# Another order of the Mamba state, its replicated loads, and VectorE's token operations interleaved

## The chip, the cores and the metric

The kernel runs on one core of one Trainium2 chip. A core has TensorE (PE) for matmuls, VectorE (DVE), ScalarE (ACT) and GpSimd (POOL) for work on elements, and SyncE (SP), which here issues nearly all DMA transfers. Each engine works through its own queue in order; semaphores join the queues. The metric is the device time of one execution in microseconds. Times of single instructions come from one profiled execution.

## The reference, cut to what matters

Four layers follow one another on x of shape (2, 128, 128, 128) in float32. Layers 0 and 2 are the same: a 3x3 convolution, then a Mamba scan in which the 128 channels of a pixel are a sequence of 8 tokens of 16 features, then a group norm, SiLU and a residual. Layer 1 gates x by a density of windows, and layer 3 is a residual block of two 3x3 convolutions with batch norm. The change lies in the scan:

```python
y = conv3x3(x, conv_w) + conv_b
seq = y.reshape(B * H * W, 8, 16)                    # 8 tokens of 16
xi, z = split(seq @ in_proj_w.T)                     # 32 channels each
xc = silu(causal_conv1d(xi))                         # over the tokens
dt, Bm, Cm = split(xc @ x_proj_w.T, [1, 17])         # Bm, Cm: 16 states
dt = softplus(dt @ dt_proj_w.T + dt_proj_b)
dA = exp(dt[..., None] * A)                          # 32 channels x 16 states
dBx = dt[..., None] * Bm[:, :, None, :] * xc[..., None]
h = a * h + b                                        # token by token
ys = sum(h * c[:, None, :], axis=-1)                 # over the 16 states
out = ((ys + D * xc) * silu(z)) @ out_proj_w.T
```

For each pixel and token there are thus 32 x 16 = 512 numbers of state.

## The kernel before, in words

The Mamba layers go through the image in tiles of four rows, 512 pixels (NS), 64 tiles a layer and 128 in all. The pixels lie along the free dimension. The 512 state numbers of a pixel are 128 partitions times 4 free groups (NJ = 4): the 32 channels are split in four groups of eight (DJ = 8, index e), and the 8 channels x 16 states of a group fill the partitions. Which partition holds channel e and state n is told by `_state(e)` (line 72). In the kernel before, states 0 to 15 of channels 0 to 6 lie at n * 7 + e, and channel 7 fills the last 16 partitions. The constants `neg` and `red` and the weights `alog` are built from the same function on the host.

Per tile k and token t the work of the scan is:

- `load` (429, SP): u = dt * xc and the pair (B, C) of the token lie in DRAM scratch (`su`, `sb`) and are read back replicated over the partitions, into `ur` (4 x 512 elements a partition, three buffers) and `bcr` (2 x 512, five buffers). Lines 435 and 439 read for the first 112 partitions, lines 436 and 440 for the last 16.
- `inject` (442, GpSimd): h(t) = ur * B, line 445, into one of four buffers.
- `decay` (447, TensorE and ScalarE): four small matmuls (line 454) spread dt * A over the partitions into two PSUM tiles named `set`, one for each half of the free groups; line 463 takes the exponential in place. There are three `set` buffers for two tiles a token, so the tiles take turns, and one that is needed again must have been read for the last time.
- `token` (465, VectorE), for each half: line 472 multiplies `set` by h(t-1) in place, line 473 multiplies the product by C into `r`, and line 477 adds the product to h(t). Below these three are called d, w and u, with the half behind: d0, w0, u0, d1, w1, u1. Token 7 has no u, and token 0 is handled apart.
- `gather` (485, TensorE): line 492 sums `r` over the states into the PSUM tile `ys`, one for four tokens; `through` (479, line 483) begins each `ys`, and `gate` (501, line 505, VectorE) takes it, twice a tile. `out` (507, line 512, TensorE) then projects, and `spread` (522) gathers statistics.

The work on the other tiles that fills the gaps is the convolution (line 323), the projections (350), dt (364, 365), softplus (368), B and C (400, 407), their product (412, GpSimd), `own` (420, 421), u (374, GpSimd), `own_u` (425 to 427) and the stores (382, 389).

The order is written by hand. Each piece of work has a place on a line of tokens: tile k's token t stands at 7k + t - 1 and so on; `put` (line 554) notes it, and everything is sorted by place and issued in that order on every engine. The places that matter here: the token operations at t - 1 for half 0 and t - 0.5 for half 1, `decay` of token t at t - 1.2, `gather` at t + 0.35, the gates at 3.79 and 7.39, `through` at 1.25 and 4.2, `out` at 7.9. In a steady tile TensorE's queue therefore has, between the matmuls of one token's `decay` and the next: for tokens 2 to 3 `out` and the second `own` of neighbouring tiles, `through`, two taps of a convolution and a `gather`; for tokens 5 to 6 two and a half projections, a `through` and a `gather`; the others have less or have waits on ScalarE in them.

Of the kernel before, what the change touches and what calls it, by code (L numbers as in the profile page):

```python
# [27 lines left out]
ALU = mybir.AluOpType  # L28
# [3 lines left out]
P = 128  # L32
NT, FT = 8, 16
DI, DS, DC = 32, 16, 4
NQ = 4
NJ = DI * DS // P
DJ = DI // NJ
NG = 4
CG = P // NG
WIN = 8  # L40
ROWS = 4
NS = ROWS * P
# [7 lines left out]
def _constants(H):  # L50

    parts = {}

    neg = np.zeros((NJ, NQ, DJ, NQ, P), np.float32)
    red = np.zeros((P, NQ, NQ, DJ), np.float32)
    gsum = np.zeros((2, NQ, DS, 2, NJ, NQ, DJ), np.float32)
    for q in range(NQ):
        for e in range(DJ):
            neg[:, q, e, q, _state(e)] = -1.0
            red[_state(e), q, q, e] = 1.0  # L60
        for g in range(2):
            gsum[g, q, :, g, :, q, :] = 1.0
    parts["neg"] = neg.reshape(P, -1)
    parts["red"] = red.reshape(P, -1)
    parts["gsum"] = gsum.reshape(P, -1)
    parts["group"] = np.kron(np.eye(NG), np.full((CG, CG), 1.0 / CG)).astype(np.float32)
    parts["ident"] = np.eye(P, dtype=np.float32)
    parts["neghalf"] = np.full((P, CG), -0.5, np.float32)
    return _packed(parts)


def _state(e):


    return np.arange(DS) + P - DS if e == DJ - 1 else np.arange(DS) * (DJ - 1) + e


def _bilinear(n):
# [38 lines left out]
def _mamba_layout(w):  # L117
# [5 lines left out]
    def half(a):  # L123

        a = a.reshape(*a.shape[:-2], 2, NQ, NJ, DJ)
        return np.ascontiguousarray(np.swapaxes(a, -3, -2)).reshape(*a.shape[:-4], 2 * P)
# [18 lines left out]
    for q in range(NQ):  # L145
        pdt1[:, q, :, :, q, :] = by_d[0][:, :, None, None]
        pdt2[:, q, :, :, q, :] = w["dt_proj_w"][:, 0].reshape(NJ, DJ)[None, None, :, :]
        pb[:, q, :, q, :] = by_d[1 : 1 + DS].transpose(1, 2, 0)
        pc[:, q, :, q, :] = by_d[1 + DS :].transpose(1, 2, 0)
        for e in range(DJ):  # L150
            alog[:, q, e, q, _state(e)] = w["A_log"].reshape(NJ, DJ, DS)[:, e, :]
# [128 lines left out]
STORE_AT = -4.15  # L280
LOAD_AT, INJECT_AT = -3.7, -1.8
REP_AT = -1.2
SUM_AT = 0.35
D_AT = (1.25, 4.2)
V_AT = (3.79, 7.39)
# [3 lines left out]
def _mamba(tc, src, w, con, dst, scratch, stats, H):  # L289


    nc = tc.nc
# [11 lines left out]
    live = {}  # L304
# [124 lines left out]
    def load(k, t):  # L429

        s = live[k]
        n = P - DS
        ur = s["ur", t] = st.tile([P, NJ, NS], F32, tag="ur", name="ur", bufs=3)
        u = s["su"][t]
        nc.sync.dma_start(out=ur[:n], in_=u[: DJ - 1].unsqueeze(0).to_broadcast([DS, DJ - 1, NJ, NS]))
        nc.sync.dma_start(out=ur[n:], in_=u[DJ - 1].unsqueeze(0).to_broadcast([DS, NJ, NS]))
        m = s["bc", t] = st.tile([P, 2, NS], F32, tag="bcr", name="bcr", bufs=5)
        b = s["sb"][t]
        nc.sync.dma_start(out=m[:n], in_=b.unsqueeze(1).to_broadcast([DS, DJ - 1, 2, NS]))
        nc.sync.dma_start(out=m[n:], in_=b)  # L440

    def inject(k, t):
        s = live[k]
# [18 lines left out]
        for x in a:  # L462
            nc.scalar.activation(x, x, AF.Exp)  # L463

    def token(k, t, jp):

        s = live[k]
        if jp == 0:
            s["r", t] = st.tile([P, NJ, NS], F32, tag="r", name="r", bufs=2)
        pt = s["a", t][jp]  # L470
        js = slice(2 * jp, 2 * jp + 2)
        nc.vector.tensor_tensor(pt, pt, s["h", t - 1][:, js, :], ALU.mult)  # L472
        nc.vector.tensor_tensor(  # L473
            s["r", t][:, js, :], pt, s["bc", t - 1][:, 1].unsqueeze(1).to_broadcast([P, 2, NS]), ALU.mult
        )
        if t < NT - 1:
            nc.vector.tensor_tensor(s["h", t][:, js, :], pt, s["h", t][:, js, :], ALU.add)  # L477

    def through(k, g):

# [66 lines left out]
    x1, z1 = ahead(1)[0], behind(1)[0]  # L547
    order = [(0, band)] + taps(0, 0, 9) + [(0, turn)] + x0 + taps(1, 0, 3) + dt0 + taps(1, 3, 5) + bc0
    order += [(0, load, 0), (0, load, 1), (0, load, 2)]
    order += z0 + taps(1, 5, 9) + [(1, turn), (0, decay, 1), (0, inject, 0), (0, inject, 1)] + own0  # L550
    order += x1[:2] + z1[:2]
    early = {x: n - 100.0 for n, x in enumerate(order)}

    def put(k, at, f, *args):
        at = early.get((k, f, *args), k * SPAN + at)
        todo.append((at, len(todo), f, (k, *args)))


    for k in range(len(src) * ntile):
        if k * ROWS % BAND == 0:  # L560
            put(k, BAND_AT, band)
        for tap in range(9):
            put(k, CONV_AT[tap], conv, tap)
        put(k, TURN_AT, turn)
        for n in range(4):
            put(k, IN_AT[n], project, *divmod(n, 2))
        for name in ("xc", "zs"):
            put(k, SILU_AT, silu, name)
        for i in range(2):
            put(k, BC_AT[i], inout, i)  # L570
        for g in range(2):
            put(k, DT_AT[g], step, g)
        put(k, SOFTPLUS_AT, softplus)
        put(k, PROD_AT, product)
        put(k, U_AT, scaled)
        for g in range(2):
            put(k, OWN_AT[g], own, g)
        put(k, OWN_U_AT, own_u)
        put(k, STORE_AT, store)
        for t in range(NT - 1):  # L580
            put(k, LOAD_AT + t, load, t)
            put(k, INJECT_AT + t, inject, t)
        for t in range(1, NT):
            put(k, REP_AT + t, decay, t)
            for jp in range(2):
                put(k, t - 1 + jp / 2, token, t, jp)
            put(k, SUM_AT + t, gather, t)
        for g in range(2):
            put(k, D_AT[g], through, g)
            put(k, V_AT[g], gate, g)  # L590
        put(k, OUT_AT, out)
        put(k, STATS_AT, spread)
        put(k, KEEP_AT, keep)
# [26 lines left out]
def _gates(tc, src, w, con, y, stats, wm, b1, up, dst, H):  # L620
# [6 lines left out]
    with tc.tile_pool(name="dg", bufs=2) as dp, tc.tile_pool(name="dg1", bufs=1) as sp, tc.tile_pool(  # L627
# [58 lines left out]
        def gram(b, y0):  # L686
# [3 lines left out]
            pg = s["pg"] = psg.tile([P, 2, 512], F32, tag="pg", name="pg")  # L690
            tiles = [(a, a * P // 2, g * CG) for g in range(NG) for a in range(2)]
            for a, pa, c0 in tiles:
# [335 lines left out]
def _program(ctx, tc, d, cols, out):  # L1028
# [7 lines left out]
    with tc.tile_pool(name="const", bufs=1) as cp, tc.tile_pool(name="wts", bufs=1) as wp:  # L1036
        cc = cols["const"]
        ct = cp.tile([P, cc["neghalf"][1]], F32, tag="ct", name="ct")
        nc.sync.dma_start(out=ct, in_=d["const"])
        con = {k: ct[:, a:b] for k, (a, b) in cc.items()}  # L1040
        w1 = cp.tile([P, CG], F32, tag="w1", name="w1")
        nc.sync.dma_start(out=w1, in_=d["w1t"])
        w2 = cp.tile([CG, 2 * P + P // 2], F32, tag="w2", name="w2")
        nc.sync.dma_start(out=w2, in_=d["w2b"])
        b1 = cp.tile([CG, 1], F32, tag="b1", name="b1")
        nc.sync.dma_start(out=b1, in_=d["b1"])
        wm = {"w1": w1, "w2": w2[:, :P], "b2": w2[:, P : 2 * P], "one": w2[:, 2 * P :]}

        y = [dram.tile([P, H, P], F32, tag=f"y_{b}", name=f"y_{b}") for b in range(B)]

        def layer(src, n):
            w = _layer_weights(nc, wp, {k: d[f"L{n}_{k}"] for k in ("conv", "fold", "alog", "keep")}, cols[n], con)
            stats = wp.tile([P, B, H // ROWS, 6], F32, tag="stats", name="stats")
            _mamba(tc, src, w, con, y, scratch, stats, H)
            return w, stats

        x = [d["x"][b] for b in range(B)]
        w, stats = layer(x, 0)
        _gates(tc, x, w, con, y, stats, wm, b1, d["up"], x2, H)
        w, stats = layer(x2, 2)  # L1060
        with tc.tile_pool(name="ps_n", bufs=1, space=PSUM) as pp:
            norm = [_norm(nc, npool, pp, w, con, stats, b) for b in range(B)]
# [44 lines left out]
```

## Time and profile before

| | |
|---|---|
| median of 3 runs | 7580.34 us (7578.54 to 7589.2) |
| span of the profiled execution | 7571.5 us |
| difference of the two | 8.8 us |
| first Mamba layer, first d to last | about 57 to 3310 us |
| second Mamba layer, first d to last | about 3655 to 6900 us |
| DMA busy share, 1000 to 3000 us | 0.97, at 250 GB/s |
| VectorE busy, 1000 to 3000 us | 1928.0 of 2000 us |
| mean granted TensorE clock | 0.929 |

The span runs from the first to the last instruction. The two Mamba layers are some 86% of it, and a tile takes about 50 us in them. Busy times count an engine's own work, not its waits; a matmul's end is modelled. A row such as "L472 DVE ... x1792 | 2193.5, 1224 | 267.6 <-ACT set L463 165.4" reads: line 472 on VectorE ran 1792 times, was busy for 2193.5 us, took 1224 ns on average, and VectorE stood idle for 267.6 us just before these instructions, 165.4 of it ended by ScalarE's line 463. In a row of order in time the first number is the start and the second the duration, both in us, and equal neighbours are merged.

### The profile page before, as it was taken

The page shows a single profiled execution, that of the slowest core. Times are in us where ns is not written, and L with a number is a line of the kernel's source. Part 1 is how long each engine was busy: PE and PEld are TensorE (multiplying, and loading weights), DVE is VectorE, ACT ScalarE, POOL GpSimd, SP SyncE. Part 2 cuts the span into 40 slices and gives each one's busy share as a digit, 9 for nine tenths or more (in the row PEclk, how much of TensorE's full clock was granted, in tenths as well). Part 3 has the DMA queues.
Part 4 walks back from the last instruction along what each step waited for, and adds up shares of the span by engine and source line. Part 5 has one row for each costly group of instructions (what it writes and reads, how often), then busy time and mean ns, then how long its engine had stood idle before and what let it go on. Part 6 is the DMA issues. An engine that isn't in the chain of part 4 may idle for free.

```text
span 7571.5 us, 89536 instructions
## 1 busy us (share of the span) xinstructions
PE 6319.0 (83%) x30416; PEld 2335.1 (31%) x30416; DVE 7011.8 (93%) x7114; ACT 4282.3 (57%) x4877; POOL 5499.8 (73%) x1783
## 2 busy tenths in 40 slices
PE   7888888888888888867788888888888888887994
PEld 2222222222222222224222222222222222223873
DVE  5999999999999999978699999999999999999986
ACT  5666666666656656545556666666656655662222
POOL 5878777877787778754578777877787778775541
PEclk8999999999999999978899999999999999997997
DMA  8999999999999999954799999999999999996604
GB/s 204 252 251 252 251 250 246 256 251 253 246 248 254 250 243 249 245 194 173 193 249 247 250 250 249 250 256 246 249 252 252 251 245 253 249 253 199 207 7 172
DMA packets 573738, 1769.80 MB, mean 234 GB/s; under 512 B 85568, under 2 KB 239712, under 8 KB 458208
## 3 DMA queue, kind: packets, MB, share of 16 engines
q1 hardware_dynamic: 568672, 1747.28, 88.1%
q10 hardware_dynamic: 4608, 16.78, 0.6%
q8 instruction: 242, 3.96, 0.2%
q14 instruction: 216, 1.77, 0.1%
HBM read 1552.83 MB, written 210.89 MB: 233 GB/s over the span
## 4 chain that ended last, share of the span: by engine, by line
DVE 41%; DMA 25%; PE 19%; issue 7%; ACT 5%; POOL 2%; SPq 1%; POOLq 0%; DVEq 0%; ACTq 0%
DMA bcr<-sb 19%; DVE set L472 14%; DVE h L477 12%; DVE r L473 12%; PE m L911 6%; DMA ur<-su 3%; PE one L350 2%; PE set L454 2%; ACT set L463 2%; PE ys L492 2%; PE one L400 2%; POOL h L445 2%; DVE v L505 1%; PE ys L483 1%; ACT xc L357 1%
## 5 line engine op out<-in xcount | busy, mean ns | idle before, releaser
L445 POOL TENSOR_TENSOR h<-ur,bcr 128x2048 f32<-128x2048 f32 x896 | 4060.7, 4539 | 1257.0 <-DMA bcr<-sb 1096.1
L472 DVE TENSOR_TENSOR set<-set,h 128x1024 f32<-128x1024 f32 x1792 | 2193.5, 1224 | 267.6 <-ACT set L463 165.4
L473 DVE TENSOR_TENSOR r<-set,bcr 128x1024 f32<-128x1024 f32 x1792 | 2194.5, 1225 | 61.5
L463 ACT ACTIVATE set<-set 128x1024 f32<-128x1024 f32 x1792 | 1745.9, 1006 | 870.0 <-PE set L454 856.6
L477 DVE TENSOR_TENSOR h<-set,h 128x1024 f32<-128x1024 f32 x1536 | 1866.0, 1215 | 28.1 <-POOL h L445 27.8
L454 PE MATMUL set<-dt,rep 32*128 32x512 f32 x7168 | 1402.9, 675 | 104.9 <-DVE h L477 98.1
L492 PE MATMUL ys<-r,ct 128*32 128x512 f32 x7168 | 1172.5, 635 | 36.4 <-DVE r L473 36.1
L323 PE MATMUL one<-band,conv 128*128 128x512 f32 x2304 | 1081.3, 605 | 21.9 <-DMA band<-in_x_dram 12.6
L454 PEld LDWEIGHTS set<-dt,rep 32*128 32x128 f32 x7168 | 405.1, 193 | 1002.3 <-issue 468.1
L400 PE MATMUL one<-xc,keep 128*64 128x512 f32 x1008 | 322.4, 723 | 462.1 <-ACT xc L357 355.5
L323 PEld LDWEIGHTS one<-band,conv 128*128 128x128 f32 x2304 | 406.6, 189 | 668.0 <-issue 596.8
L911 PE MATMUL m<-comb,u 128*128 128x256 f32 x2304 | 507.8, 381 | 46.0 <-DVE comb L904 44.8
L483 PE MATMUL ys<-t,ct 128*128 128x512 f32 x512 | 322.6, 716 | 252.3 <-DVE v L505 250.7
L911 PEld LDWEIGHTS m<-comb,u 128*128 128x128 f32 x2304 | 436.2, 190 | 117.3 <-issue 54.5
L492 PEld LDWEIGHTS ys<-r,ct 128*32 128x32 f32 x7168 | 181.2, 112 | 929.2 <-issue 759.6
L352 ACT ACTIVATE xc<-one,keep 128x512 f32<-128x512 f32 x252 | 173.4, 688 | 509.2 <-PE one L350 504.2
L374 POOL TENSOR_TENSOR u<-dt,xc 128x1024 f32<-128x1024 f32 x128 | 302.8, 2365 | 98.0 <-ACT dt L368 98.0
L420 PE MATMUL one<-prod,ct 128*128 128x512 f32 x504 | 280.8, 640 | 109.1 <-POOL prod L412 78.8
L350 PE MATMUL one<-y,w_in 128*128 128x512 f32 x504 | 341.1, 765 | 1.6 <-ACT xc L352 1.6
L463 ACT ACT_TABLE_LOAD x254 | 325.9, 1283 | 4.5
L427 POOL TENSOR_TENSOR t<-t,xc 128x1024 f32<-128x1024 f32 x128 | 302.4, 2363 | 10.0
L364 PE MATMUL one<-xc,w_dt 128*128 128x512 f32 x504 | 306.4, 692 | 2.7 <-ACT bc L407 2.7
(167 smaller groups left out, 5901.7 us busy)
## 6 DMA issues: line engine op xcount, KB each, us to landing
ur<-su SPq DMA_DIRECT2D x896, 896.0 KB, 11.5
bcr<-sb SPq DMA_DIRECT2D x896, 448.0 KB, 11.7
ur<-su SPq DMA_DIRECT2D x896, 128.0 KB, 11.1
su<-u SPq DMA_DIRECT2D x1024, 64.0 KB, 3.4
sb<-bc SPq DMA_DIRECT2D x256, 224.0 KB, 2.7
bcr<-sb SPq DMA_DIRECT2D x896, 64.0 KB, 11.0
y<-o SPq DMA_DIRECT2D x128, 256.0 KB, 9.3
band<-in_x_dram SPq DMA_DIRECT2D x28, 640.0 KB, 10.9
```

What stands on the lines that cost most here:

```text
L323: nc.tensor.matmul(py.rearrange("p (r w) -> p r w", r=ROWS), lhsT=w["conv"][:, tap, :], rhs=xb[:, r + kh : r + kh + ROWS, kw : kw + P], st ...
L350: nc.tensor.matmul(p, lhsT=w[("in", "z")[i]][:, g, :], rhs=s["y"], start=True, stop=True)
L400: nc.tensor.matmul(p[g * NQ * DS : (g + 1) * NQ * DS, :], lhsT=w[("xb", "xcm")[i]], rhs=s["xc"][:, g, :], start=True, stop=True,)
L445: nc.gpsimd.tensor_tensor(b, s["ur", t], s["bc", t][:, 0].unsqueeze(1).to_broadcast([P, NJ, NS]), ALU.mult)
L454: nc.tensor.matmul(a[j // 2][:, j % 2, :], lhsT=w["rep"][r, q, :], rhs=s["dt"][r, g, :], start=True, stop=True, tile_position=(r.start, 0),)
L463: nc.scalar.activation(x, x, AF.Exp)
L472: nc.vector.tensor_tensor(pt, pt, s["h", t - 1][:, js, :], ALU.mult)
L473: nc.vector.tensor_tensor(s["r", t][:, js, :], pt, s["bc", t - 1][:, 1].unsqueeze(1).to_broadcast([P, 2, NS]), ALU.mult)
L477: nc.vector.tensor_tensor(s["h", t][:, js, :], pt, s["h", t][:, js, :], ALU.add)
L483: nc.tensor.matmul(s["ys", g], lhsT=con["ident"], rhs=s["t1"][:, g, :], start=True, stop=False)
L492: nc.tensor.matmul(s["ys", g][a : a + NQ * DJ, :], lhsT=red[:, q, :], rhs=r[:, j, :], start=False, stop=(q == NQ - 1), tile_position=(0, a),)
L911: nc.tensor.matmul(m[:, n // 2, n % 2], lhsT=u[:, i, kw, :], rhs=v[:, i, :, kw : kw + P], start=(kw == 0), stop=(kw == 2),)
```

## The change

It has two parts. First, `_state` is another order: the 128 partitions are two halves of 64, one for channels 0 to 3 and one for channels 4 to 7; inside a half each state has four neighbouring partitions, one for each channel. `load` is rewritten to fit: bcr comes by two transfers of 32 partitions (eight states of the lower half each) and one of 64 (all 16 states of the upper half), ur by two of 64 partitions. They are issued in the order bcr 0 to 31, bcr 32 to 63, ur upper half, ur lower half, bcr upper half. That is five transfers a token where there were four, for the same bytes.

Second, `token` is cut in three functions with places of their own, so that VectorE's queue has d0, u1 of the token before, w0, d1, u0, w1 in a steady token, where it had d0, w0, u0, d1, w1, u1. The second gate of a tile comes after w0 of token 1 and the first one after u0 of token 4.

```diff
+NE = DJ // 2
 def _state(e):
-    return np.arange(DS) + P - DS if e == DJ - 1 else np.arange(DS) * (DJ - 1) + e
+    return P // 2 * (e // NE) + NE * np.arange(DS) + e % NE
...
+TOKEN_AT = (("decayed", (0.0, 0.5)), ("weighted", (0.34, 0.84)), ("update", (0.67, 1.17)))
...
     def load(k, t):
         s = live[k]
-        n = P - DS
+        half, part = P // 2, P // 4
         ur = s["ur", t] = st.tile([P, NJ, NS], F32, tag="ur", name="ur", bufs=3)
-        u = s["su"][t]
-        nc.sync.dma_start(out=ur[:n], in_=u[: DJ - 1].unsqueeze(0).to_broadcast([DS, DJ - 1, NJ, NS]))
-        nc.sync.dma_start(out=ur[n:], in_=u[DJ - 1].unsqueeze(0).to_broadcast([DS, NJ, NS]))
         m = s["bc", t] = st.tile([P, 2, NS], F32, tag="bcr", name="bcr", bufs=5)
-        b = s["sb"][t]
-        nc.sync.dma_start(out=m[:n], in_=b.unsqueeze(1).to_broadcast([DS, DJ - 1, 2, NS]))
-        nc.sync.dma_start(out=m[n:], in_=b)
+        u, b = s["su"][t], s["sb"][t]
+        for at in (0, part):
+            rows = b[at // NE : (at + part) // NE]
+            nc.sync.dma_start(
+                out=m[at : at + part], in_=rows.unsqueeze(1).to_broadcast([part // NE, NE, 2, NS])
+            )
+        for at, e in ((half, NE), (0, 0)):
+            nc.sync.dma_start(
+                out=ur[at : at + half], in_=u[e : e + NE].unsqueeze(0).to_broadcast([DS, NE, NJ, NS])
+            )
+        nc.sync.dma_start(out=m[half:], in_=b.unsqueeze(1).to_broadcast([DS, NE, 2, NS]))
...
-    def token(k, t, jp):
+    def decayed(k, t, jp):
+        s = live[k]
+        pt = s["a", t][jp]
+        nc.vector.tensor_tensor(pt, pt, s["h", t - 1][:, 2 * jp : 2 * jp + 2, :], ALU.mult)
+    def weighted(k, t, jp):
...
+    def update(k, t, jp):
+        s = live[k]
+        h = s["h", t][:, 2 * jp : 2 * jp + 2, :]
+        nc.vector.tensor_tensor(h, s["a", t][jp], h, ALU.add)
...
-            for jp in range(2):
-                put(k, t - 1 + jp / 2, token, t, jp)
+            for f, at in TOKEN_AT:
+                for jp in range(2):
+                    if f != "update" or t < NT - 1:
+                        put(k, t - 1 + at[jp], {"decayed": decayed, "weighted": weighted, "update": update}[f], t, jp)
```

## The prediction

> **What bounds the kernel now.** I read the busy line first, then the costliest groups, VectorE's order in time, who waits for whom, and TensorE's order in time.
>
> ```profile
> PE 6319.0 (83%) x30416; PEld 2335.1 (31%) x30416; DVE 7011.8 (93%) x7114; ACT 4282.3 (57%) x4877; POOL 5499.8 (73%) x1783
> ...
> L445 POOL TENSOR_TENSOR h<-ur,bcr 128x2048 f32<-128x2048 f32 x896 | 4060.7, 4539 | 1257.0 <-DMA bcr<-sb 1096.1
> L472 DVE TENSOR_TENSOR set<-set,h 128x1024 f32<-128x1024 f32 x1792 | 2193.5, 1224 | 267.6 <-ACT set L463 165.4
> L473 DVE TENSOR_TENSOR r<-set,bcr 128x1024 f32<-128x1024 f32 x1792 | 2194.5, 1225 | 61.5
> ...
> L477 DVE TENSOR_TENSOR h<-set,h 128x1024 f32<-128x1024 f32 x1536 | 1866.0, 1215 | 28.1 <-POOL h L445 27.8
> ```
>
> VectorE is the fullest engine, and three lines, 472 (d), 473 (w) and 477 (u), are most of it. GpSimd waits 1096.1 us for replicated loads, but VectorE waits for GpSimd only 97.2 us at line 472 (two waits, the fills of the two layers) and 27.8 us at line 477. The loads are nearly saturated and still not the bound; the median h is ready 7 to 12 us before the next token's d.
>
> VectorE in order of time (start, duration):
>
> ```profile
> 2090.07 1.23 DVE L473 TENSOR_TENSOR r<-set,bcr 128x1024 f32<-128x1024 f32 x1
> 2091.21 1.22 DVE L477 TENSOR_TENSOR h<-set,h 128x1024 f32<-128x1024 f32 x1
> 2092.34 1.22 DVE L472 TENSOR_TENSOR set<-set,h 128x1024 f32<-128x1024 f32 x1
> 2093.60 1.23 DVE L473 TENSOR_TENSOR r<-set,bcr 128x1024 f32<-128x1024 f32 x1
> ```
>
> From w to u it is 1.14 us start to start, from u to d 1.13, from d to w 1.26 (medians over all pairs: 1.141, 1.131, 1.257). An instruction starts some 0.085 us before its forerunner ends, unless it reads what that forerunner wrote; then it starts 0.034 after. u reads d's result two places on and pays nothing.
>
> A tile of VectorE work: 14 d x 1.257 + 14 w x 1.141 + 12 u x 1.131 + two gates x 0.598 + statistics 0.600 = 48.94 us. The trace's mean tile (first d to first d, 114 tiles away from both ends of the layers) is 50.43. The other 1.49 us are waits of d for ScalarE's exponentials:
>
> ```profile
> PE ys L483 <- DVE v L505: 250.7, 128, 2.9
> ...
> DVE set L472 <- ACT set L463: 165.4, 185, 9.3
> ```
>
> Each line ends with the total, the number of waits and the longest. The first line is how one of the second arises: TensorE stands at line 483 until VectorE's gate v is done, and the exponential of token 6 comes late.
>
> **The change, VectorE's order.** It was d0 w0 u0 d1 w1 u1 in each token. It becomes d0 u1' w0 d1 u0 w1 (u1' of the token before). Every reader is now two places behind its writer, but for two pairs a tile: d0,w0 of token 1 (there is no u before it) and d1,w1 of token 7 (it has no u). So 12 d a tile cost 1.141 and not 1.257: 12 x 0.116 = 1.40 us, and the tile's VectorE work is 47.54.
>
> **What it pushes back.** u is the last reader of a PSUM tile `set`, of which there are three for two a token. Half 1 of token t+1 takes the one that u0 of token t frees, and u0 moves from third to fifth in its token. Behind the waiting matmul (line 454) on TensorE's queue stands everything up to the next token's matmuls. The heaviest such stretch follows token 2's (start, duration):
>
> ```profile
> 2087.35 2.22 PE L454 MATMUL set<-dt,rep 32*128 32x512 f32 x8
> 2089.50 2.05 PE L512 MATMUL po<-keep,v 128*128 128x128 f32 x16
> 2091.39 1.02 PE L420 MATMUL one<-prod,ct 128*128 128x512 f32 x2
> 2092.25 1.10 PE L483 MATMUL ys<-t,ct 128*128 128x512 f32 x2
> 2093.19 1.88 PE L323 MATMUL one<-band,conv 128*128 128x512 f32 x4
> 2095.01 1.06 PE L492 MATMUL ys<-r,ct 128*32 128x512 f32 x8
> 2096.00 1.14 PE L454 MATMUL set<-dt,rep 32*128 32x512 f32 x8
> ...
> 2097.18 1.93 ACT L463 ACTIVATE set<-set 128x1024 f32<-128x1024 f32 x2 [0.47 <-PE set L454]
> ```
>
> There is no idle time in it. From the second half's matmuls of token 2 (2088.45) to token 3's it is 7.55 us (the 10th and 90th percentile over the tiles agree), then 1.18 to the exponential and 1.00 for it.
>
> - Now: d0 of token 1 starts at 2084.68, u0 ends 3.62 later, and the matmul starts 0.15 after that, TensorE being busy until then. 3.77 + 7.55 + 1.18 + 1.00 = 13.50; d0 of token 3 starts at 14.72. Cover: 1.22 us.
> - After: u0 of token 1 is behind d0 (1.257), w0 (1.14), v (0.60), d1 (1.14) and lasts 1.215: 5.35. Plus 0.05 for the wait, 7.55, 1.18, 1.00 and 0.04 = 15.17. VectorE alone would start d0 of token 3 at 6.41 + 6.82 = 13.23. **A new wait of 1.94 us a tile.**
>
> The same sum elsewhere in the tile: v of token 4 now stands one w earlier, so the matmul at line 483 no longer waits and the late exponential of token 6 arrives just in time (6.75 us after token 5's d0, needed at 6.82). For token 7 ScalarE sets the time: exp1 of token 6 starts 0.18 us after d0 of token 6 (its `set` is freed by the later u0), and from its start to the end of exp0 of token 7 the trace has 7.96; 8.14 to 8.26 against VectorE's 7.42 gives a wait of 0.84. The remaining tokens keep 1 us or more. Tile: 47.54 + 1.94 + 0.84 = **50.32 us at full clock**, 0.11 below today's mean.
>
> **The clock.** TensorE stands idle more before that long stretch: its first half's matmuls end 3.1 us after d0 of token 1 and the next may start at 5.40, about 2.2 us. What such a wait does, in stretches of 3.41 us (first number TensorE busy, then the granted clock after POOL):
>
> ```profile
> core 0: us, PE busy (x) PEld busy (x) DVE busy (x) ACT busy (x) POOL busy (x), PEclk, DMA share, GB/s
> ...
> 2112.24:2115.66 3.42, 1.48 (x5) 0.68 (x4) 3.38 (x5) 0.76 (x2) 3.42 (x2) 1.00 0.68 197
> 2115.66:2119.07 3.41, 3.41 (x11) 0.70 (x10) 3.38 (x4) 0.69 (x1) 2.92 (x1) 0.50 0.98 293
> ```
>
> 1.48 busy of 3.42 (57% idle) is followed by one stretch at clock 0.50. In the first Mamba stage 44 full-clock stretches of 56 to 58% idle did this in 9 cases of 10, 33 with 48 to 56% never. All half-clock records are multiples of 3.41 us on one grid. A wait of 2.2 us puts 1.9 us or more into one stretch for about (3.41 - 2.2 + 2 x 0.3)/3.41, or half, of its positions. Each costs 3.41/2 = 1.7 us of the 7.55 us chain, which has no cover left: 0.5 x 1.7 = 0.9. **Tile 51.2.** Bounds: never (50.32), always (52.0); I take half, by the positions.
>
> [...]
>
> **The loads.** Five transfers a token and not four, the same bytes: 128 packets of 8 KB (ur) and 128 of 4 KB (bcr). SP issues at about 0.57 us each, 7 x 0.57 = 4.0 us more a tile; behind them on SP stand the stores of u, bc and o and the band loads, and GpSimd waits for the result; its lead of 7 us or more covers that, and without it the 4.0 us would be on the path. In the packet records of the Mamba stage an 8 KB packet takes 498 ns (median), a 4 KB one 259, with 309 and 159 at the fast end; in the last stage 4 KB packets take 159 with 14.1 of 16 engines at work. Some 8 KB packets take 1.2 us, four times the fast end. [...] But each of the two small bcr transfers has eight blocks; if they run on eight engines, those carry 8 + 12 packets a token and not 8 + 8. Bounds: 8 x 0.309 + 12 x 0.159 + 0.92 (other traffic, from its shares) = 5.3 us, or with no relief 8 x 0.498 + 12 x 0.259 + 0.92 = 8.0. I take the lower half, about 6, since the fast value is what a regular shape reaches; under 7.2 a token it is hidden. What it then yields: shorter fills (0 to 10 us in all; I take 7) and the ragged tiles (50.43 against 50.33 for the regular four-tile pattern 50.9, 48.9, 51.4, 50.1): 0.1 x 126 = 13.
>
> [...]
>
> **Sum.** 126 tile periods x (51.2 - 50.43 = 0.77) = +97; loads -7 - 13; net +77 on the profiled 7571.5, and with the 8.8 us by which the median run is longer, 7580 + 77, about **7660 us**. At full clock throughout: 126 x -0.11 - 20 = -34, 7546. Half clock in every tile: 126 x 1.57 - 20 = +178, 7758. The forecast's own range is 7546 to 7758.
>
> **Rivals.**
> - *Full clock throughout* (18%): 7546, as above, if TensorE's wait falls short of 1.9 us of one stretch. For: only 2.2 us; against: other short gaps lie beside it.
> - *The gain arrives* (12%): the new wait at token 3 doesn't form, because TensorE takes up later work before the matmul or the buffers rotate otherwise. Tile 47.54 + 0.84 = 48.4: 126 x -2.05 - 20 = 7300. Against: today that matmul starts within 0.15 us of u0's end.
> - *The loads become the bound* (8%), on the slow side: eight engines with 12 small packets and no relief, 8.0 x 7 = 56 us a tile, +5.6 x 126: 8280. It decides from 7.3 us a token. Against: the 159 ns packets.
> - *The order doesn't close the gap* (5%): each w still pays 0.116, some 10 a tile outside the stretch that ends in the new wait: 51.2 + 1.2 = 52.4, 7810. Against: u, two places behind d, pays nothing.
>
> The forecast holds 57%. A change under 0.2% (15 us) can't be told from none. Faster 0.29 (most of the full clock and the gain), same 0.08, slower 0.63. The range 7530 to 7820 leaves out the gain and the loads, 2 in 10.
>
> **What would show it.** d to w 1.14 start to start in 12 of 14; line 472's wait for ACT up from 165 to 350 us or more, nearly all at tokens 3 and 7; matmuls at 454 waiting for u (98.1 and the weight loads' 335.7 us) much longer, those at 483 for v (250.7) nearly gone; DMA share well under 0.97 and GpSimd's 1096 us a fraction. I am wrong if token 3's d doesn't wait, or if GpSimd's wait grows.

## The result and the profile after

The changed kernel takes 8080.04 us (median of 4 runs, 8076.47 to 8082.95), the kernel before 7584.77 in the same session: a ratio of 1.0644, 95% interval 1.0627 to 1.0662. It is slower by 6.4%, and the forecast, 7660 with a range of 7530 to 7820, is missed. The profiled execution spans 8081.2 us. The tile periods explain it: the mean tile, first d to first d away from the layers' ends, went from 50.44 to 54.61 us, and all 126 periods, those at a layer's ends included, went from 6397.5 to 6900.0 us together: 502 of the 510 us of span.

In the changed code d is line 476, w 483, u 494, the decay matmuls 461, the exponential 470, GpSimd's inject 452, B and C 402. The busy line and the groups that answer to those of before:

```profile
PE 6895.6 (85%) x30416; PEld 2636.7 (33%) x30416; DVE 6893.1 (85%) x7114; ACT 4310.2 (53%) x4877; POOL 5492.0 (68%) x1783
...
L452 POOL TENSOR_TENSOR h<-ur,bcr 128x2048 f32<-128x2048 f32 x896 | 4055.3, 4536 | 794.4 <-DMA bcr<-sb 588.2
L476 DVE TENSOR_TENSOR set<-set,h 128x1024 f32<-128x1024 f32 x1792 | 2196.5, 1226 | 966.6 <-ACT set L470 863.3
...
L483 DVE TENSOR_TENSOR r<-set,bcr 128x1024 f32<-128x1024 f32 x1792 | 2176.7, 1215 | 8.8
L461 PE MATMUL set<-dt,rep 32*128 32x512 f32 x7168 | 1760.7, 713 | 436.9 <-DVE h L494 421.7
L494 DVE TENSOR_TENSOR h<-set,h 128x1024 f32<-128x1024 f32 x1536 | 1863.3, 1213 | 9.2 <-POOL h L452 9.2
```

VectorE worked 119 us less (7011.8 to 6893.1), but waited 863.3 us for exponentials where it had waited 165.4. It still hardly waits for GpSimd. TensorE's decay matmuls were busy for 1760.7 us, against 1402.9 for the same 7168 before: part of it is the clock (a record that starts at half clock takes 1056 ns at the median, at full clock 662), part that a half which stands alone takes 1.13 us, as long as both together (1.14 at 1718.31). VectorE in order of time, from the first d of a tile:

```profile
1703.62 1.23 DVE L476 TENSOR_TENSOR set<-set,h 128x1024 f32<-128x1024 f32 x1 [1.42 <-ACT set L470]
...
1706.62 1.22 DVE L476 TENSOR_TENSOR set<-set,h 128x1024 f32<-128x1024 f32 x1
1707.75 1.22 DVE L494 TENSOR_TENSOR h<-set,h 128x1024 f32<-128x1024 f32 x1
1708.88 1.22 DVE L483 TENSOR_TENSOR r<-set,bcr 128x1024 f32<-128x1024 f32 x1
1710.02 1.22 DVE L476 TENSOR_TENSOR set<-set,h 128x1024 f32<-128x1024 f32 x1
...
1720.52 1.23 DVE L476 TENSOR_TENSOR set<-set,h 128x1024 f32<-128x1024 f32 x1 [3.63 <-ACT set L470]
```

From d to u to w to d it is 1.13 us start to start: the gap that a dependent neighbour paid (1.257) is closed, as forecast. Then token 3's d waits 3.63 us, where 1.94 were forecast at full clock. It starts 16.90 us after token 1's d; the forecast chain was 15.17, and the 1.73 more is about what one half-clock stretch costs (an estimate: 3.41 / 2 = 1.71). TensorE in the same place:

```profile
1706.19 1.13 PE L461 MATMUL set<-dt,rep 32*128 32x512 f32 x4
1709.12 1.13 PE L461 MATMUL set<-dt,rep 32*128 32x512 f32 x4 [1.79 <-DVE h L494]
1710.17 3.52 PE L529 MATMUL po<-keep,v 128*128 128x128 f32 x16
```

It stands between the halves of token 2's decay, for u0 of token 1, and the 16 matmuls of `out`, 2.05 us before, now take 3.52.

Nearly all steady tiles are alike, 54.60 to 54.62 us, which is 16 x 3.413. Four of the 16 stretches are at half clock in each of them. In stretches of 3.41 us (first number after the comma TensorE busy, granted clock after POOL):

```profile
core 0: us, PE busy (x) PEld busy (x) DVE busy (x) ACT busy (x) POOL busy (x), PEclk, DMA share, GB/s
1707.07:1710.49 3.42, 1.63 (x8) 0.65 (x7) 3.42 (x4) 1.22 (x2) 3.42 (x2) 1.00 0.81 244
1710.49:1713.90 3.41, 3.41 (x17) 3.34 (x16) 3.41 (x4) 0.96 (x2) 1.88 (x1) 0.50 0.49 147
1724.14:1727.55 3.41, 2.13 (x9) 0.57 (x9) 3.41 (x4) 1.01 (x1) 3.33 (x3) 1.00 0.87 231
1727.55:1730.97 3.42, 3.42 (x4) 1.37 (x5) 3.42 (x4) 1.01 (x1) 3.42 (x2) 0.50 0.60 175
1734.38:1737.79 3.41, 2.72 (x9) 0.97 (x6) 2.57 (x3) 2.52 (x3) 3.41 (x1) 1.00 0.90 202
1737.79:1741.21 3.42, 3.42 (x16) 0.76 (x14) 3.42 (x4) 1.27 (x2) 0.58 (x1) 1.00 1.07 243
1748.03:1751.45 3.42, 3.42 (x9) 1.13 (x10) 2.56 (x3) 3.10 (x4) 2.27 (x1) 0.50 1.03 220
1751.45:1754.86 3.41, 3.41 (x10) 0.33 (x9) 3.41 (x4) 1.43 (x2) 2.24 (x1) 0.50 1.13 244
```

The first pair comes near the rule of the prediction without fitting it (52% idle, then half; among its rows 48 to 56% idle never did that). The second is far from it: 38% idle, and half all the same. After the third, 20% idle, the clock stays. The last pair has TensorE busy throughout at half clock, and it stays at half. So idle time doesn't tell which stretches these are.

A measure that may tell can be worked out from the matmul records: give each matmul its streaming time (records of 512 columns start 0.429 us apart at the median, line 325 at full clock) times the part of the array that it uses, with the 128 rows and 128 columns of the largest matmuls in the rows as the whole. A decay matmul has 32 rows, a quarter; a gather 32 columns, a quarter. Four of a decay's records run side by side when both halves are issued together (at 1718.31 four start within 0.02 us, and the eight take 1.14 us), but only two when a half stands alone (at 1706.19 two start within 0.01 us, and the four take 1.13), so a decay cut in two by a wait uses half of the array for twice the time. **Theory C:** a stretch that used less than some 0.35 to 0.40 of the array's time is followed by half clock.

### The profile page after: what moved, and what is told of

Its sections match the earlier page's. It is cut to its first block, busy times and chain, and to the rows that moved or that the text cites. A ratio compares the mean times of both kernels' runs of the same rounds, so it can differ in the third digit from the quotient of the medians.

```text
span 8081.2 us, 93386 instructions
## 1 busy us (share of the span) xinstructions
PE 6895.6 (85%) x30416; PEld 2636.7 (33%) x30416; DVE 6893.1 (85%) x7114; ACT 4310.2 (53%) x4877; POOL 5492.0 (68%) x1783
## 4 chain that ended last, share of the span: by engine, by line
PE 41%; DVE 21%; DMA 16%; issue 9%; ACT 6%; SPq 5%; POOL 1%; DVEq 0%; ACTq 0%; POOLq 0%
PE set L461 11%; DVE set L476 8%; DVE h L494 7%; DMA bcr<-sb 7%; PE one L325 6%; PE m L930 6%; DMA ur<-su 5%; PE ys L509 5%; DVE r L483 4%; PE po L529 3%; ACT set L470 3%; PE one L352 3%; PE one L402 2%; PE one L366 2%; SPq L440 2%
## 5 line engine op out<-in xcount | busy, mean ns | idle before, releaser
L452 POOL TENSOR_TENSOR h<-ur,bcr 128x2048 f32<-128x2048 f32 x896 | 4055.3, 4536 | 794.4 <-DMA bcr<-sb 588.2
L476 DVE TENSOR_TENSOR set<-set,h 128x1024 f32<-128x1024 f32 x1792 | 2196.5, 1226 | 966.6 <-ACT set L470 863.3
L461 PE MATMUL set<-dt,rep 32*128 32x512 f32 x7168 | 1760.7, 713 | 436.9 <-DVE h L494 421.7
L325 PE MATMUL one<-band,conv 128*128 128x512 f32 x2304 | 1287.6, 702 | 21.8 <-DMA band<-in_x_dram 11.9
L509 PE MATMUL ys<-r,ct 128*32 128x512 f32 x7168 | 1074.3, 672 | 1.9 <-DVE r L483 1.9
L461 PEld LDWEIGHTS set<-dt,rep 32*128 32x128 f32 x7168 | 489.5, 197 | 1504.7 <-issue 1031.8
L325 PEld LDWEIGHTS one<-band,conv 128*128 128x128 f32 x2304 | 477.0, 222 | 804.4 <-issue 723.9
L414 POOL TENSOR_TENSOR prod<-bc 128x512 f32<-128x512 f32 x128 | 162.3, 1268 | 512.1 <-ACT bc L409 498.6
L529 PE MATMUL po<-keep,v 128*128 128x128 f32 x2048 | 439.9, 404 | 1.3 <-DVE v L522 1.3
L529 PEld LDWEIGHTS po<-keep,v 128*128 128x128 f32 x2048 | 403.6, 302 | 105.5 <-issue 101.3
L366 PE MATMUL one<-xc,w_dt 128*128 128x512 f32 x504 | 400.4, 887 | 2.7 <-ACT bc L409 2.7
L352 PE MATMUL one<-y,w_in 128*128 128x512 f32 x504 | 286.2, 650 | 82.1 <-ACT xc L354 82.1
```

What stands on the lines that cost most here:

```text
L325: nc.tensor.matmul(py.rearrange("p (r w) -> p r w", r=ROWS), lhsT=w["conv"][:, tap, :], rhs=xb[:, r + kh : r + kh + ROWS, kw : kw + P], st ...
L352: nc.tensor.matmul(p, lhsT=w[("in", "z")[i]][:, g, :], rhs=s["y"], start=True, stop=True)
L366: nc.tensor.matmul(p, lhsT=w["dt"], rhs=s["xc"][:, g, :], start=True, stop=True)
L452: nc.gpsimd.tensor_tensor(b, s["ur", t], s["bc", t][:, 0].unsqueeze(1).to_broadcast([P, NJ, NS]), ALU.mult)
L461: nc.tensor.matmul(a[j // 2][:, j % 2, :], lhsT=w["rep"][r, q, :], rhs=s["dt"][r, g, :], start=True, stop=True, tile_position=(r.start, 0),)
L476: nc.vector.tensor_tensor(pt, pt, s["h", t - 1][:, 2 * jp : 2 * jp + 2, :], ALU.mult)
```

## The experiments

Two questions come first: which part costs the time, and by what.

**1. The order alone, the loads alone.** `order_alone` is the changed kernel with `_state` and `load` of before; `loads_alone` is the new `_state` and `load` with `token` of before.

> VectorE's new order with the old state order and the old four loads a token. Theory A (the new order makes TensorE stand between the two halves of a decay, and the half-clock stretches that follow it lengthen the tile to 54.6 us): 8080 us, 8000 to 8150, line 476's counterpart waits 800 us or more for ACT, granted clock about 0.87. Rival B (the new loads or the new state order cost the time): near 7580, clock 0.93.

> The new state order and the five new loads with VectorE's old order. Theory A: 7540 to 7585 us (the tile stays at 50.3 to 50.4 us, clock 0.93, GpSimd's wait for the loads well under 1096 us). Rival B (loads): near 8080. If the regular load pattern makes the tile regular, the lower end.

Measured: `order_alone` takes 8078.88 us (ratio 1.0653, interval 1.0618 to 1.0687), tile 54.61, clock 0.866, the very waits of the changed kernel:

```profile
DVE set L471 <- ACT set L465: 863.4, 499, 10.3
...
POOL h L447 <- DMA bcr<-sb: 111.9, 42, 14.2
```

`loads_alone` takes 7896.03 (1.0415, 1.0384 to 1.0446), tile 53.09 on average. Each part alone makes the kernel slower, and the two don't add: the order's limit lies just above the loads' one and hides it. Theory A holds for the order; of the loads both theories were wrong. `loads_alone`:

```profile
L451 POOL TENSOR_TENSOR h<-ur,bcr 128x2048 f32<-128x2048 f32 x896 | 4057.4, 4535 | 1693.3 <-DMA bcr<-sb 1247.9 <-DMA ur<-su 198.1 <-DVE r L479 90.8
...
L483 DVE TENSOR_TENSOR h<-set,h 128x1024 f32<-128x1024 f32 x1536 | 1867.4, 1216 | 221.5 <-POOL h L451 220.9
```

VectorE now waits for GpSimd at u (220.9 us against 27.8 before), and GpSimd for the loads. If the loads set this tile, a token's loads take 53.09 / 7 = 7.58 us. GpSimd's wait for bcr, 588.2 us in the changed kernel, is only 111.9 in `order_alone` (the second row above) with the same tile length: the old loads serve that tile with ease, the new ones just manage.

**2. Filling TensorE's waits, first in the wrong place.** The same number of matmuls is added where TensorE stands, with 128 rows of the array or with 32. If idle time sets the clock, both must help; if the array's share does, only the first.

```diff
+        for _ in range({3: 3, 5: 2}.get(t, 0)):
+            nc.tensor.matmul(
+                a[0][:, 0, :], lhsT=w["rep"][:128, q, :], rhs=s["dt"][:128, g, :], start=True, stop=True
+            )
         for j in range(NJ):
```

> The changed kernel plus five more matmuls a tile, which sit where TensorE stands between the two halves of the decays of tokens 3 (1.79 us idle, three matmuls of 0.52 us) and 5 (1.28 us idle, two matmuls); each uses all 128 rows of the array, and what it writes is overwritten at once. Theory C (the clock of a 3.41 us stretch goes by how much of the array the stretch before used, a 32-row matmul counting a quarter): two of the four half-clock stretches of a tile go, tile 51 to 53 us, 7630 to 7880 us. Theory D (the clock goes by TensorE's idle time, whatever the matmuls are): the same. Theory E (the waits alone make the tile, the clock only shows them): 8080 or more, since work is added.

> The same five matmuls at the same places, with the same 512 columns and the same duration, but with 32 of the 128 rows of the array. Theory C (share of the array): almost no help, 8020 to 8100 us. Theory D (idle time): the same gain as with 128 rows, 7630 to 7880. Theory E: 8080 or more.

Measured: 8506.93 (1.1218, 1.1189 to 1.1248) and 8485.91 (1.1194, 1.1163 to 1.1224). A miss of mine, twice over: the decays that stand between their halves are those of tokens 2 and 4, not 3 and 5, and such a matmul makes two records of 0.43 us, not one of 0.52. So 10 x 0.43 = 4.3 us of work a tile lay in the chain and not in its gaps; the tile rose by 3.2 to 3.4. The granted clock rose alike in both (0.909 and 0.907), which speaks neither for C nor against it: in these runs, too, 144 of 144 and 133 of 133 full-clock stretches under 0.35 of the array's time were followed by half clock.

**3. Filling them in the right place.** Two matmuls for token 2, one for token 4, and two before the first matmul at line 402, where TensorE stands for 2.05 us.

```diff
+        for _ in range({2: 2, 4: 1}.get(t, 0)):
+            nc.tensor.matmul(
+                a[0][:, 0, :], lhsT=w["rep"][:128, q, :], rhs=s["dt"][:128, g, :], start=True, stop=True
+            )
...
         p = one(k)
+        for _ in range(0 if i else 2):
+            nc.tensor.matmul(p, lhsT=w["rep"][:128, 0, :], rhs=s["y"][:128], start=True, stop=True)
```

> The changed kernel plus five matmuls a tile (0.86 us each) at the places where TensorE really stands: two before the first half of token 2's decay (1.79 us idle behind it), one before token 4's (1.28 us), two before the first matmul at line 402 (2.05 us); 128 rows of the array, results overwritten at once. Theory C (the clock goes by the share of the array in use): most of the four half-clock stretches of a tile go, tile 50.3 to 52.5 us, 7540 to 7820 us. Theory D (idle time): the same. Theory E (waits alone, the clock only shows them): 8080 or more.

> The same five matmuls at the same places, of the same length, with 32 of the 128 rows. Theory C: they add 0.06 to 0.13 of a stretch's array time where 0.25 to 0.5 would be added by 128 rows, so most stretches stay under about 0.36 and the half clock stays: 7900 to 8100 us, clock under 0.90. Theory D (idle time): the same gain as with 128 rows. Theory E: 8080 or more.

Measured: with 128 rows 7918.42 us (1.0448, 1.0432 to 1.0465) at a clock of 0.950, 0.87 half stretches a tile in the first Mamba stage; with 32 rows 8065.0 (1.063, 1.0606 to 1.0653) at 0.895, three a tile, the tile again at 54.61. Theory E, by which the clock only shows the waits, falls with the first: it needed 8080 or more. The rows of `refill_32rows`:

```profile
1711.51:1714.92 3.41, 3.15 (x9) 1.14 (x8) 3.41 (x5) 0.79 (x2) 2.48 (x2) 1.00 0.91 247
1714.92:1718.33 3.41, 3.19 (x9) 1.72 (x10) 3.41 (x5) 1.81 (x2) 3.41 (x1) 0.50 0.97 213
1731.99:1735.40 3.41, 2.98 (x11) 1.00 (x8) 3.41 (x4) 1.29 (x2) 3.33 (x3) 1.00 0.61 185
1735.40:1738.81 3.41, 3.41 (x5) 1.33 (x4) 3.41 (x4) 0.72 (x1) 3.41 (x2) 0.50 0.31 82
1742.23:1745.64 3.41, 2.72 (x6) 0.88 (x6) 2.57 (x4) 2.52 (x3) 3.41 (x1) 1.00 1.00 226
1745.64:1749.05 3.41, 3.40 (x15) 0.75 (x14) 3.41 (x4) 1.27 (x2) 2.21 (x2) 1.00 0.97 333
```

Stretches in which TensorE was busy for 3.15 and 2.98 of 3.41 us are followed by half clock, one with 2.72, less, is not: theory D falls, and C stands. The same counting over the first Mamba stage of all 18 traces of this case gives, for stretches at full clock:

```
share of the array's time used    stretches    followed by half clock
under 0.35                         1239          1234
0.35 to 0.40                        368           159
0.40 and more                     10408             0
```

The two fills differ in rows only, so the rows alone could be what counts. Other measures settle that. In a slightly wider count of the same stages (14,618 full-clock stretches), the best single limit on the array's share puts 114 stretches on the wrong side; on the rows alone it is 553, on TensorE's idle time 612, on the columns alone 872.

The 128-row run, though, fell short of the clock's worth (7540 to 7820 were expected), and GpSimd waits 1271.1 us for bcr in it: the loads again.

**4. Both limits away.** The new order, the 128-row fill, and the loads and state of before.

> The new VectorE order with the old state order and the old loads, plus the five 128-row fill matmuls a tile. With the new loads this fill gave 7918 us at a granted clock of 0.95, with GpSimd waiting 1271 us for bcr. Theory F (two limits lie one behind the other: the clock at 54.6 us a tile, and the new loads at about 53): without either the tile is what the waits alone give, 50.3 to 50.9 us; 7550 to 7640 us. Rival G (the fill itself or the waits of the new order, not the loads, held that run): 7880 to 7950 again.

Measured: 7607.6 us (1.0026, 1.0011 to 1.0042), as theory F has it: two limits lay one behind the other. Hardly a stretch is at half clock (0.02 a tile in the first Mamba stage), the median tile is 50.42 us (the mean 50.66, as some are longer), and the two waits left in the median tile are the forecast ones:

```profile
1700.14 1.23 DVE L477 TENSOR_TENSOR set<-set,h 128x1024 f32<-128x1024 f32 x1 [2.00 <-ACT set L471]
...
1729.50 1.23 DVE L477 TENSOR_TENSOR set<-set,h 128x1024 f32<-128x1024 f32 x1 [0.93 <-ACT set L471]
```

These are the d of tokens 3 and 7; 1.94 and 0.84 us were worked out for them.

**5. Why the new loads are slower.** Over 1000 to 3000 us, from the packet records:

```
                 8 KB packet   4 KB packet   8 or 9 packets   16 or more
                 median ns     median ns     under way        under way
before              498           259          under 1%          85%
loads_alone         465           244          12%               70%
loads_even          586           268          under 1%          88%
loads_whole         586           280          under 1%          89%
```

With the new loads a packet is a little faster, but for an eighth of the time only 8 or 9 packets are under way, as if half of the 16 engines had none. The sum of the prediction for engines that carry both small bcr transfers, with these medians, is 8 x 0.465 + 12 x 0.244 + 0.92 = 7.57 us a token, the 7.58 measured. `loads_even` replaces the two by one transfer of 64 partitions; `loads_whole` numbers the state n * 8 + e, so that ur and bcr come in one transfer of 128 partitions each. The edit of the first:

```diff
-        for at in (0, part):
-            rows = b[at // NE : (at + part) // NE]
-            nc.sync.dma_start(
-                out=m[at : at + part], in_=rows.unsqueeze(1).to_broadcast([part // NE, NE, 2, NS])
-            )
+        nc.sync.dma_start(out=m[:half], in_=b.unsqueeze(1).to_broadcast([DS, NE, 2, NS]))
```

> The new state order and loads with VectorE's old order, but bcr's lower half comes in one 64-partition transfer instead of two of 32. Theory L (each 32-partition bcr transfer runs on only half of the DMA engines, which then carry 8 + 12 packets a token: 8 x 0.465 + 12 x 0.245 + 0.92 = 7.58 us, 53.1 a tile, against the 52.9 that the new loads alone showed): with even halves 8 x 0.465 + 8 x 0.245 + 0.92 = 6.6 us a token, 46 a tile, hidden again; 7540 to 7590 us, mean DMA share up or GpSimd's wait for bcr well under 1248 us. Rival M (half-height transfers of ur or the new state order itself are slow): stays at 7850 to 7900.

> VectorE's old order; the state numbered channel by channel (8 channels of a state number next to each other) so that ur and bcr come in one transfer of 128 partitions each, two a token. Theory P (what is slow is that a transfer of 64 partitions keeps all engines on one half of the partitions: 16 engines moved an 8 KB packet in 586 ns there, 8 engines in 311): packets spread over both halves get nearer to 309 and 159 ns; the loads are hidden, 7520 to 7590 us, GpSimd's wait well under 1096 us. Rival Q (the replicated reading is slow, or where the 8 packets of an engine lie makes no difference): 8 KB packets at 498 ns or more, 7580 to 8150.

Measured: 8138.61 (1.0726, 1.0701 to 1.0751), tile 55.17, and 8014.74 (1.056, 1.054 to 1.0579), tile 54.05; GpSimd waits 1624.8 and 1561.8 us for bcr. For `loads_even` both theories fell; for `loads_whole` theory P fell and its rival Q held. About 16 packets are now under way nearly all the time, and an 8 KB packet takes 586 ns, not 465; 8 x 0.586 + 8 x 0.268 + 0.92 = 7.75 us comes near the 55.17 / 7 = 7.88. So the arithmetic of theory L held, and its assumption, that packets keep their time, didn't: with the two small transfers packets are faster and fewer are under way, without them more are under way and packets are slow. That a transfer has only 64 partitions is not the cause either, since 128 are as slow (586 ns in both).

No run here shows which engine carried a packet or took which partition; why the old loads are the best of the four stays open.

**6. Other orders.** In the first, u0 comes before d1: d0 u1' w0 u0 d1 w1. It ran with the even loads (`early_u0`) and with the old ones; `places_retuned` has d0 d1 w0 u0 w1 u1 and other places for the work between.

```diff
-TOKEN_AT = (("decayed", (0.0, 0.5)), ("weighted", (0.34, 0.84)), ("update", (0.67, 1.17)))
+TOKEN_AT = (("decayed", (0.0, 0.6)), ("weighted", (0.3, 0.8)), ("update", (0.45, 1.15)))
```

> VectorE's order d0 u1' w0 u0 d1 w1 (u0 fourth instead of fifth, next to its w), with bcr in two even halves. u0 frees its buffer about 1.1 us earlier than in the changed kernel, and only one pair a token is closer than two places. Theory A with C (the late u0 and the clock it costs made the loss) and theory L: tile 49 to 50 us, 7400 to 7530 us. If the loads stay slow (rival M): 7850 or more. If any interleaving loses: 8000.

> VectorE's order d0 u1' w0 u0 d1 w1 with the old state order and the old loads. Theory F (the 8152 us of this order with even half-height loads were the loads'): u0 is early enough that TensorE stands less; tile 49.3 to 50 us, 7420 to 7530, faster than both. Rival (this order, too, loses by itself): 8000 or more.

> Old loads; VectorE's order d0 d1 w0 u0 w1 u1 (every reader two places behind its writer but w0,u0's own chain, which has none) and the places of the other work moved so that TensorE's work lies more evenly between the decays (TURN -10.41, BC -8.41 and -8.16, DT -7.21 and -7.07, OWN -6.39 and -5.97, U -4.85, OWN_U -3.25, INJECT -2.45 and some tenths elsewhere). If buffers and clock are what hold the order, the tile nears VectorE's own 47.5 us and then the old loads (15.5 of 16 engines busy at 50.4 us) are the bound at 49 to 50: 7400 to 7530 us. If not, 7600 or more.

Measured: 8152.29 (1.0751), the even loads' limit again; 7581.42 with the old loads (0.9996, 0.9978 to 1.0014), no different from before and not the 7420 to 7530 expected; and 7716.52 (1.0172, 1.0137 to 1.0208), slower. The last one's tile runs from 48.15 to 57.34 us (10th and 90th percentile), 1.9 half stretches each; which of its many moves is to blame stays open.

**7. Do the old loads hold the tile at 50.4?** Before, `early_u0_old_loads` and `order_refill` had profiled spans within 10 us of each other. In the kernels called light, three of seven ur loads of a tile are left out, as the first expectation says:

```diff
+        if t % 2:
+            s["ur", t] = s["ur", t - 1]
+        else:
+            ur = s["ur", t] = st.tile([P, NJ, NS], F32, tag="ur", name="ur", bufs=3)
...
```

> The kernel before, with ur loaded for even tokens only (odd tokens use the tile of the token before: 3 of 7 ur loads a tile are left out, and the output is another). Theory H (the old loads hold the tile at 50.4 us): tile 49 to 49.6 us, 7390 to 7470 us. Theory I (waits for exponentials and the clock hold it, as the trace's rows say): 7520 to 7580, a little of it shorter fills.

> VectorE's order d0 u1' w0 u0 d1 w1, old loads, with the same 3 of 7 ur loads left out. Theory H: tile 49 to 49.6 us, 7380 to 7470 us. Theory I: 7520 to 7580, clock still about 0.93.

> Order d0 u1' w0 u0 d1 w1, old loads complete, plus two 128-row matmuls of 0.86 us before the first one at line 402, where TensorE stands 1.86 us a tile. Theory I: the half-clock stretches go and the tile nears VectorE's own 48.7 us: 7380 to 7460 us, clock 0.96 or more, faster than before. Theory H: 7550 to 7600, clock up, GpSimd's wait for bcr the same.

> The same with 3 of 7 ur loads left out. Both theories: tile 48.3 to 49 us, 7330 to 7440 us; theory H differs from I only in that early_u0_refill is then 100 us or more slower than this.

Measured: 7527.32 (0.9931, 0.9912 to 0.9951), 7445.07 (0.9824, 0.9801 to 0.9846), 7581.35 (1.0003, 0.9991 to 1.0016) and 7441.13 (0.9816, 0.9797 to 0.9835). For the kernel before theory I holds: tile 50.2 instead of 50.4, held by exponentials and clock. For the early u0 theory H holds: 49.5 instead of 50.5, so its saving is there and the loads take it back. (With the loads their issues on SP are left out too; which of the two counts isn't shown.) What their lateness looks like on VectorE, first with all loads, then with fewer:

```profile
DVE set L471 <- ACT set L465: 284.6, 228, 10.8
DVE set L471 <- POOL h L447: 99.2, 2, 53.9
DVE h L489 <- POOL h L447: 41.6, 48, 3.7
```

```profile
DVE set L474 <- ACT set L468: 199.8, 130, 9.9
DVE set L474 <- POOL h L450: 99.8, 2, 54.8
...
DVE h L492 <- POOL h L450: 4.0, 2, 2.0
```

The u's waits for GpSimd go, and with them 30% of the waits for exponentials; that u's lateness had made these through the `set` buffers fits, but isn't shown. The fill at line 402 brings nothing in either; the two kernels with it are 140 us apart, as theory H has it, though the lighter one's tile, 49.5, lies above the 48.3 to 49 expected. No complete kernel tried here beats the one before by more than its measurement can tell; an order that does needs loads that take under some 7 us a token (an estimate: 49.5 / 7 = 7.1).

## Why the prediction was wrong, point by point

- *VectorE's order saves 1.40 us a tile.* Right: 1.13 us from neighbour to neighbour, two pairs a tile at 1.257. Tile less waits is 54.61 - 6.75 = 47.86 us; 47.54 was forecast.
- *u0's lateness makes TensorE stand at token 2's second half, and d waits 1.94 at token 3 and 0.84 at token 7; 50.32 us at full clock.* Right, mechanism and size, as the median tile of `order_refill` shows: 2.00, 0.93, 50.42.
- ***The failed step: "0.5 x 1.7 = 0.9" for the clock.*** The mechanism, a wait that brings a half-clock stretch into a chain without cover, was right. The size was 54.61 - 50.42 = 4.2 us a tile. `order_alone` and `order_refill`, which differ by the fill alone, are 471 us apart (8078.88 - 7607.6), nearly the whole loss of 495. Three things in the step were wrong. It went by idle time, 56%, where the share of the array tells the stretches apart (10,408 at 0.40 or more, none followed by half clock; 1239 under 0.35, all but five); so token 4's split decay (38% idle) and a half-clock stretch full of small matmuls were not counted. Only the one place at token 2 was looked at, and there are three, with four stretches. And "half of its positions" took the positions as spread evenly, while the tile's length settled at 16 stretches, with the same four slow in each. The waits that this adds are 1.69 us at token 3, 0.84 at token 5 and 1.42 at token 1. The upper bound, one slow stretch in every tile (52.0), was thus no bound.
- *The loads: about 6 us a token, hidden, a gain of 20 us in all.* Wrong, but without effect here. No run shows that a regular shape brings the fast packets of 309 and 159 ns; at the median packets took 465 and 244 in `loads_alone`, 586 and 268 or 280 with the other two new shapes. Alone the loads take 7.58, if they set the tile of that run, within the bounds of 5.3 to 8.0 and near the end that was not taken; the eight engines with 8 + 12 packets were named and then waved off. The rival "the loads become the bound", with its limit of 7.3 us a token, is what `loads_alone` shows. In the changed kernel GpSimd's wait is half as long as before, one of the signs named for fast loads; but `order_alone` shows that a longer tile does that by itself.

## What to carry to other kernels

A wait that is priced at full clock must be priced again at the clock it causes (token 3's d: 1.94 us at full clock, 3.63 measured), and by the share of the array that the matmuls around it use: the same small matmuls use less of the array in a stretch when a wait cuts them apart than side by side (here the four records of half a decay took 1.13 us alone, the eight of a whole one 1.14). When a period can lock to the clock's grid, as here at 16 stretches, a cost can be paid in every period, so an average over positions is no forecast, and its bounds must count every gap of the period. Two changes that are both slower can hide each other: run each alone, and judge a transfer's new shape by packet time and by packets under way together.

## What the runs showed of the hardware

The clock followed the array's use in all 18 traces: of 10,408 full-clock stretches with 0.40 or more of the array's time used none was followed by half clock (1 of 12,709 in the wider count), of 1239 under 0.35 all but five were; so was one with TensorE 92% busy (3.15 of 3.41 us, `refill_32rows`). The half-clock stretches whose matmuls used less than 0.65 of the array's time were all followed by half clock again (372 of 372); records of 512 columns started 0.853 us apart there and 0.429 at full clock (line 325 of the changed kernel, medians). An 8 KB replicated packet took 586 ns at the median in both runs whose transfers filled 64 partitions or 128, with some 16 packets under way, 498 with transfers of 112 and 16, and 309 in `loads_alone` while 8 or 9 packets were under way.
